# Experts: the last 96 rows of the down product, taken four tiles at a time in 32-row groups

## The chip, the core and the metric

The kernel runs on one core of a Trainium2 chip. A core has five engines with queues of their own: TensorE (PE in the profile; PEld is its weight load), VectorE (DVE), ScalarE (ACT), GpSimd (POOL) and SyncE (SP), and 16 DMA engines. The metric is the time of one execution on the device in microseconds; lower is better. The kernel before takes 3897.37 us, the median of 13 runs (3891.37 to 3909.9).

## The reference

One decoder layer in float32 on x of 32 x 128 x 512: a self-attention, a cross-attention and a mixture of experts, each with a residual. The part that matters here is the mixture. There are T = 4096 tokens of E = 512 features; each goes to 6 of 32 experts:

```python
g = jax.lax.ragged_dot(xs, w_gate, group_sizes)      # 512 -> 352, by expert
u = jax.lax.ragged_dot(xs, w_up, group_sizes)        # 512 -> 352
d = jax.lax.ragged_dot(jax.nn.silu(g) * u, w_down, group_sizes)   # 352 -> 512
expert_out = jnp.sum(out * weights[..., None], axis=1)            # out: d in token order
shared = jax.nn.silu(x @ sw_gate) * (x @ sw_up) @ sw_down
```

The contraction of the down product is over M = 352 = 128 + 128 + 96 rows. TensorE contracts over up to 128 partitions at a time, so the last piece fills 96 of them.

## The kernel before, in words

The 4096 x 6 assignments are sorted by expert into tiles of 128 tokens; `usual` = 4096 x 6 / 128 + 32 / 2 = 208 tiles are always run, and a second part for more of them stands under a condition. Class `Experts` runs them in a loop over i. There are four sets of weights (SETS = 4): tile i uses set i % 4, and a new expert's weights are loaded only if the tile's expert is new to its set (`cond=new`).

For each tile:

- `tokens` (line 1415): POOL gathers the tile's 128 token rows from DRAM in four indirect DMAs (L1421) into `e_xr` (three buffers). It is called for tile i + 5 in iteration i.
- `turn_in`: VectorE transposes them into `e_xT` (L1433), for tile i + 2 in iteration i.
- `gate_up`: TensorE makes gate and up, four matmuls each (L1446), in the two banks of one PSUM tile; there are four such PSUM tiles (`psum`, bufs=4) for the whole kernel. ACT takes Silu of gate (L1450), VectorE multiplies it by up into `e_gu` (L1451), and ACT's queue issues a DMA that writes it to DRAM (L1453).
- `part_out`: ACT's queue issues the DMA that reads it back in another layout, `e_gr` (L1462); it waits until the write has landed. A row count of 96 x 4 = 384 is kept for 352 values, the rest being zero from a memset.
- `turn_out`: VectorE transposes it into `e_guT` (L1472, two instructions: 96 partitions and 32 partitions), for tile i - 1 in iteration i.
- `down` (line 1477): TensorE makes the down product of tile i - 2 in three matmuls of 128, 128 and 96 rows (L1482) into one bank; ACT scales the result by the tokens' weights into `e_y` (L1486, two buffers); POOL adds the rows to `sum_d` in DRAM with an indirect DMA that accumulates (L1487). All these scatter-adds write the same tensor.
- `weights_in` and `weights_out`: SP's queue issues the loads of the three weights, gate and up after the tile that used the set before, the two parts of down after its down product.

The engines' queues are strictly in the order of the calls for PE, DVE, ACT and POOL (`manual_schedule` in `run`, line 1507); SP's order is a scheduler's, held by the waits. An instruction that waits holds up everything behind it in its queue. The order of calls in one iteration of the loop before is:

```python
self.gate_up(i)
self.turn_in(i + 2)
self.turn_out(i - 1)
self.weights_in(i + SETS)
self.down(i - 2)
self.weights_out(i - 2 + SETS)
self.part_out(i)
self.tokens(i + 5)
```

After the expert stage `Shared.group` runs five more groups of the shared expert; they read `sum_d` and write the output. It contains matmuls over 64 rows that stand in pairs on two halves of the partitions (L1253) after full ones (L1246). The cross-attention earlier has matmuls over 32 rows (L690 and L713).

Of the kernel before, what the change touches and what calls it, by code (L numbers as in the profile page):

```python
# [18 lines left out]
P = 128  # L19
# [1244 lines left out]
class Experts:  # L1264
# [9 lines left out]


    Q = 4
    RUN = 96

    def __init__(
        self, cm, ctx, table_ds, h3_d, sum_d, w_gate, w_up, w_down, eid, fresh, rows, n_tiles  # L1280
    ):
        self.cm, self.h3_d, self.sum_d, self.eid, self.fresh = cm, h3_d, sum_d, eid, fresh
        self.w_in, self.w_out, self.n_tiles = (w_gate, w_up), w_down, n_tiles
        nc, tc = cm.nc, cm.tc

# [12 lines left out]
        self.wd = [cp.tile([P, len(M_CHUNKS), E], F32, name=f"wd{s}") for s in range(SETS)]  # L1298

        self.gu_s = cp.tile([P, self.Q * self.RUN], F32, name="e_gu")  # L1300

        self.row_i = cp.tile([P, 2], I32, name="e_row_i")
        self.row = cp.tile([P, 2], F32, name="e_row")
        self.last, self.expert = None, {}
        self.got, self.spread = {}, {}
        self.xr, self.xT, self.gu, self.gr, self.guT = {}, {}, {}, {}, {}

    def fetch(self):
# [17 lines left out]
        nc.gpsimd.memset(self.gu_s, 0.0)  # L1326
        nc.gpsimd.iota(self.row_i, pattern=[[0, 2]], base=self.T + 1, channel_multiplier=1)

    def arrange(self, j):
# [69 lines left out]
    def weights_out(self, i):  # L1399

        if i >= self.end:
            return
        e, new = self.expert.pop(i)
        wd, src = self.wd[i % SETS], self.w_out[ds(e, 1)]
        top = (self.Q - 1) * 32
        m = (self.Q - 1) * self.RUN
        self.cm.nc.sync.dma_start(
            out=wd[0:top], in_=src[:, 0:m, :].rearrange("o (p c) m -> p (o c) m", p=top), cond=new
        )
        self.last = self.cm.nc.sync.dma_start(  # L1410
            out=wd[top:P, 0:2, :], in_=src[:, m:M, :].rearrange("o (p c) m -> p (o c) m", c=2),
            cond=new,
        )

# [23 lines left out]
    def gate_up(self, i):  # L1438
        if i >= self.end:
            return  # L1440
        nc = self.cm.nc
        pgu = self.cm.banks()
        t, s = self.xT.pop(i), i % SETS
        for half, w in enumerate((self.wg[s], self.wu[s])):
            for c in range(EC):
                nc.tensor.matmul(  # L1446
                    pgu[:, half, 0:M], t[:, c, :], w[:, c, :], start=c == 0, stop=c == EC - 1
                )
# [3 lines left out]
        self.gu[i] = self.dram.tile([self.Q, P, self.RUN], F32, name="e_gu_d")  # L1452
        nc.scalar.dma_start(  # L1453
            out=self.gu[i].rearrange("q s m -> s q m"),
            in_=self.gu_s.rearrange("s (q m) -> s q m", q=self.Q),
        )

    def part_out(self, i):


        gr = self.gr[i] = self.p2.tile([P, self.Q, self.RUN], F32, name="e_gr")
        self.cm.nc.scalar.dma_start(  # L1462
            out=gr.rearrange("p t m -> p (t m)"),
            in_=self.gu.pop(i).rearrange("q (i t) m -> (q i) (t m)", t=self.Q),
        )

    def turn_out(self, i):
        g = self.gr.pop(i)
        t = self.guT[i] = self.p2.tile([P, len(M_CHUNKS), P], F32, name="e_guT")
        top = (self.Q - 1) * 32  # L1470
        for rows, n in ((slice(0, top), 3), (slice(top, P), 2)):
            self.cm.nc.vector.transpose(  # L1472
                t[rows, 0:n, :].rearrange("p c (t i) -> p c t i", t=self.Q),
                g[rows, :, 0 : 32 * n].rearrange("p t (j c) -> p c t j", c=n),
            )

    def down(self, i):
        nc = self.cm.nc
        py = self.cm.banks()[:, 0, :]
        t, s = self.guT.pop(i), i % SETS  # L1480
        for c, (_, n) in enumerate(M_CHUNKS):
            nc.tensor.matmul(  # L1482
                py, t[:n, c, :], self.wd[s][:n, c, :], start=c == 0, stop=c == len(M_CHUNKS) - 1
            )
        y = self.p2.tile([P, E], F32, name="e_y")
        nc.scalar.mul(y, py, self.weight[:, i : i + 1])  # L1486
        nc.gpsimd.indirect_dma_start(  # L1487
            out=self.sum_d[:, :],
            out_offset=bass.IndirectOffsetOnAxis(ap=self.into[:, i : i + 1], axis=0),
# [5 lines left out]

    def begin(self, first, end):

        self.first, self.end, self.last = first, end, None
        for i in range(first, first + SETS):
            self.weights_in(i)  # L1500
            self.weights_out(i)

    def first_tokens(self):
        for i in range(self.first, self.first + 3):
# [2 lines left out]
    def run(self):  # L1507
# [3 lines left out]
        with self.cm.tc.manual_schedule(engines={en.PE, en.DVE, en.Activation, en.Pool}):  # L1511
            for i in range(first, first + 2):
                self.turn_in(i)
                self.tokens(i + 3)
            for i in range(first, self.end + 2):
                self.gate_up(i)
                self.turn_in(i + 2)
# [3 lines left out]
                if i > first + 1:  # L1521
                    self.down(i - 2)
                    self.weights_out(i - 2 + SETS)
                if i < self.end:
                    self.part_out(i)
                self.tokens(i + 5)


@with_exitstack
# [179 lines left out]
```

## Time and profile before

| what | value |
|---|---|
| median of 13 runs | 3897.37 us (3891.37 to 3909.9) |
| the profiled execution | 3896.81 us |
| its span, first to last instruction | 3895.1 us |
| granted TensorE clock, mean | 0.992 |
| PE busy in the span | 3778.8 us, 97% |
| POOL busy in the span | 2354.3 us, 60% |
| L1446, gate and up, 2 x 1664 records | 527.9 and 526.4 us |
| L1482, down, 1248 records | 570.5 us |
| L1421, gathers, x832 | 851.5 us, 1023 ns each |
| L1487, scatter-adds, x208 | 336.0 us, 1615 ns each |

A float32 matmul leaves two records in this trace: 208 tiles x 3 down matmuls are 1248 records. Busy time leaves out register, semaphore and DMA-issuing instructions, and the time an engine needs between two instructions is shown as idle time, put down to "issue". Because matmuls are pipelined, the length of a group of them is read best from the start of the next group, and not from its own length.

### The profile page before, as it was taken

To read this page: it belongs to the slowest core of one execution; us is meant where nothing else is said; L and a number is where in the kernel's file an instruction comes from. 1 tells how busy PE (TensorE), PEld (TensorE's weight loads), DVE (VectorE), ACT (ScalarE), POOL (GpSimd) and SP (SyncE) were. 2 spreads that over 40 slices of the span, in tenths; PEclk is the share of its full clock that TensorE was granted. 3 is DMA by queue.
4 is the path that set the end of the run, shared out by engine and by line. 5 is a ranking of instruction groups with operands and counts; after the bars stand their busy time and mean duration, and the time that the engine had idled before them with its cause. 6 is when DMAs were issued, how large, how long until landed. Compare 5 with 4: busy or idle time off the path is not lost. (4 is left out here: it accounts for less than half of the span.)

```text
span 3895.1 us, 58185 instructions
## 1 busy us (share of the span) xinstructions
PE 3778.8 (97%) x19060; PEld 2013.7 (52%) x19060; DVE 2056.6 (53%) x3202; ACT 1682.6 (43%) x4032; POOL 2354.3 (60%) x2582
## 2 busy tenths in 40 slices
PE   8999999989999999999999999999999999999999
PEld 5666666534444444444445555555555555555444
DVE  5788777777787777778223333333333333333111
ACT  6888888857677676776301111111111111111000
POOL 3545544545777777776336777777777777775000
PEclk9999999999999999999999999999999999999999
DMA  3111110121111111111245767676766676676210
GB/s 111 33 34 34 34 34 28 34 87 49 58 58 45 49 50 50 50 50 36 68 145 141 179 165 179 145 193 152 178 159 166 169 184 156 171 171 155 83 62 32
DMA packets 285987, 387.21 MB, mean 99 GB/s; under 512 B 147888, under 2 KB 179248, under 8 KB 285616
## 3 DMA queue, kind: packets, MB, share of 16 engines
q1 hardware_dynamic: 81792, 190.98, 15.1%
q0 software_dynamic: 62912, 109.85, 14.9%
q10 hardware_dynamic: 140976, 82.60, 7.5%
q8 instruction: 154, 2.52, 0.3%
q14 instruction: 153, 1.25, 0.1%
HBM read 617.52 MB, written 143.07 MB: 195 GB/s over the span
## 5 line engine op out<-in xcount | busy, mean ns | idle before, releaser
L1421 POOL DMA_INDIRECT e_xr<-h_d,e_run_of x832 | 851.5, 1023 | 287.2 <-issue 270.6
L694 DVE TENSOR_REDUCE nm<-ps 128x2 f32<-128x1024 f32 x512 | 611.0, 1216 | 111.9 <-PE ps L690 105.3
L717 ACT ACTIVATE xp<-ps 128x1024 f32<-128x1024 f32 x512 | 506.0, 1021 | 264.9 <-PE ps L690 203.2
L1451 DVE TENSOR_TENSOR e_gu<-e_act,ps 128x352 f32<-128x352 f32 x208 | 108.4, 521 | 947.3 <-ACT e_act L1450 624.3
L1482 PE MATMUL ps<-wd,e_guT 128*128 128x512 f32 (+1 forms) x1248 | 570.5, 593 | 6.8 <-issue 5.1
L713 PE MATMUL ps<-xqn,xk 32*128 32x512 f32 x2048 | 527.1, 620 | 20.6 <-ACT xp L717 19.2
L1446 PE MATMUL ps<-wg,e_xT 128*128 128x352 f32 x1664 | 527.9, 460 | 6.6 <-DMA wg<-in_L_ffn_w_gate_dram 6.6
L690 PE MATMUL ps<-xk,xq 32*128 32x512 f32 x2048 | 527.6, 630 | 1.1 <-DVE nm L694 1.0
L1446 PE MATMUL ps<-wu,e_xT 128*128 128x352 f32 x1664 | 526.4, 459 | 0.7 <-DMA wu<-in_L_ffn_w_up_dram 0.7
L1450 ACT ACTIVATE e_act<-ps 128x352 f32<-128x352 f32 x208 | 96.5, 464 | 922.5 <-PE ps L1446 524.6
L1446 PEld LDWEIGHTS ps<-wg,e_xT 128*128 128x128 f32 x1664 | 315.0, 190 | 241.4 <-issue 107.2
L1487 POOL DMA_INDIRECT sum_d<-e_y,e_into x208 | 336.0, 1615 | 123.9 <-issue 89.9
L1446 PEld LDWEIGHTS ps<-wu,e_xT 128*128 128x128 f32 x1664 | 316.0, 190 | 177.5 <-DMA wu<-in_L_ffn_w_up_dram 2.2
L279 ACT ACTIVATE s<-s,a_nm 128x128 f32<-128x128 f32 x1024 | 395.5, 394 | 5.2 <-DVE a_nm L265 5.2
L1482 PEld LDWEIGHTS ps<-wd,e_guT 128*128 128x128 f32 (+1 forms) x1248 | 236.6, 190 | 253.7 <-issue 212.6
L713 PEld LDWEIGHTS ps<-xqn,xk 32*128 32x128 f32 x2048 | 168.6, 183 | 284.3 <-ACT xp L717 123.3
L1486 ACT ACTIVATE e_y<-ps,e_weight 128x512 f32<-128x512 f32 x208 | 143.0, 687 | 393.7 <-PE ps L1482 289.3
L228 POOL TENSOR_SCALAR k<-kz,a_keep,a_extra 128x256 f32<-128x256 f32 x128 | 82.6, 655 | 315.7 <-ACT kz L227 315.7
L1472 DVE STREAM_TRANSPOSE e_guT<-e_gr 96x384 f32<-96x384 f32 (+1 forms) x416 | 230.3, 554 | 54.8 <-DMA e_gr<-e_gu_d 38.7
L1027 POOL DMA_INDIRECT table_d<-entry,at x192 | 202.5, 1055 | 63.5 <-issue 52.8
L728 PE MATMUL ps<-xp,v 128*32 128x512 f32 x2048 | 233.0, 595 | 7.9 <-ACT xp L717 7.9
L1433 DVE STREAM_TRANSPOSE e_xT<-e_xr 128x512 f32<-128x512 f32 x208 | 226.5, 1089 | 10.6 <-DMA e_xr<-h_d,e_run_of 10.5
(272 smaller groups left out, 5289.7 us busy)
## 6 DMA issues: line engine op xcount, KB each, us to landing
wg<-in_L_ffn_w_gate_dram SPq DMA_DIRECT2D x208, 704.0 KB
wu<-in_L_ffn_w_up_dram SPq DMA_DIRECT2D x208, 704.0 KB
wd<-in_L_ffn_w_down_dram SPq DMA_DIRECT2D x208, 576.0 KB
e_gu_d<-e_gu ACTq DMA_DIRECT2D x208, 192.0 KB
e_gr<-e_gu_d ACTq DMA_DIRECT2D x208, 192.0 KB
wd<-in_L_ffn_w_down_dram SPq DMA_DIRECT2D x208, 128.0 KB
e_xr<-h_d,e_run_of POOLq DMA_INDIRECT x832
xres<-in_x_dram SPq DMA_DIRECT2D x32, 256.0 KB
```

The costliest lines, as they stand in the source:

```text
L279: nc.scalar.activation(s[:, j, c, side, :], s[:, j, c, side, :], AF.Exp, bias=nm[n][:, side, at : at + 1], accum_out=sm[n][:, to : to + 1],)
L690: self.nc.tensor.matmul(sc[:, i, :], q[rows, ts(c, P)], k[rows, :], start=True, stop=True)
L694: self.nc.vector.tensor_reduce(at[:, self.ROW[side], 2 * pair : 2 * pair + 2], sc, AX.X, ALU.max, negate=True)
L713: self.nc.tensor.matmul(sc[:, i, :], k[rows, ts(c, P)], q[rows, :], start=True, stop=True)
L717: self.nc.scalar.activation(e, sc, AF.Exp)
L728: self.nc.tensor.matmul(po[b, side][ts(j, 32), :], self.v2[b % 2][:, c, 2 * j + side, :], es[j // 2][:, j % 2, :], start=c == 0, stop=c == ...
L1421: self.cm.nc.gpsimd.indirect_dma_start(out=xr[:, t, :], out_offset=None, in_=self.h3_d.rearrange("t (q f) -> (t q) f", q=self.Q), in_offse ...
L1433: self.cm.nc.vector.transpose(xT.rearrange("p c (t i) -> p c t i", t=self.Q), self.xr.pop(i).rearrange("p t (j c) -> p c t j", c=EC),)
L1446: nc.tensor.matmul(pgu[:, half, 0:M], t[:, c, :], w[:, c, :], start=c == 0, stop=c == EC - 1)
L1472: self.cm.nc.vector.transpose(t[rows, 0:n, :].rearrange("p c (t i) -> p c t i", t=self.Q), g[rows, :, 0 : 32 * n].rearrange("p t (j c) -> ...
L1482: nc.tensor.matmul(py, t[:n, c, :], self.wd[s][:n, c, :], start=c == 0, stop=c == len(M_CHUNKS) - 1)
L1487: nc.gpsimd.indirect_dma_start(out=self.sum_d[:, :], out_offset=bass.IndirectOffsetOnAxis(ap=self.into[:, i : i + 1], axis=0), in_=y[:, :] ...
```

## The change

The first 256 rows of the down product stay per tile, as two full matmuls of 128 rows. The last 96 rows (`END` = 256, `LEFT` = 96) are laid on 32 partitions in three chunks: tile i uses the 32 partitions of its lane, i % 4, in three new tiles shared by four tiles: `wd_ends` (weights), `e_lr` (gate times up, read back) and `e_endT` (transposed). When the fourth tile of a group has had its two full matmuls (or at the end), `ends_down` does three rounds, one for each chunk, of four matmuls, one for each tile, each on its own 32 partitions and into its own bank. Until then the four tiles keep their banks: two PSUM tiles of two banks each.

What follows from it in the other queues:

- ACT's queue issues four DMAs per tile around `e_gu` in place of two: the 256 columns and the 96 columns are written and read back separately. There is no padding and no memset any more.
- VectorE transposes 128 partitions (256 columns) and 32 partitions (384 columns) in place of 96 and 32.
- SP loads the down weights as 256 rows (`weights_out`) and, after the group's last round, 96 rows for each of four tiles (`ends_in`).
- Scaling and scatter-add are taken out of `down` into `leave`. It is called up to twice in an iteration, from the list `done` of tiles whose product is complete: once between `part_out` and `tokens`, once after `tokens`. So the four tiles of a group leave in two iterations, two in each; in the other two iterations none leaves.

```diff
-    RUN = 96
+    RUN = 64
+    END, LEFT = 256, 96
...
-        self.wd = [cp.tile([P, len(M_CHUNKS), E], F32, name=f"wd{s}") for s in range(SETS)]
-
-        self.gu_s = cp.tile([P, self.Q * self.RUN], F32, name="e_gu")
+        self.wd = [cp.tile([P, self.END // P, E], F32, name=f"wd{s}") for s in range(SETS)]
+        self.ends = cp.tile([P, self.LEFT // 32, E], F32, name="wd_ends")
+        self.lr = cp.tile([P, self.Q, self.LEFT], F32, name="e_lr")
+        self.gu_s = cp.tile([P, M], F32, name="e_gu")
...
+    def ends_in(self, i):
+        if i >= self.end:
+            return
         e, new = self.expert.pop(i)
...
+            out=self.ends[ts(i % SETS, 32)],
+            in_=self.w_out[ds(e, 1)][:, self.END : M, :].rearrange("o (p c) m -> p (o c) m", p=32),
             cond=new,
...
         nc.scalar.dma_start(
-            out=self.gu[i].rearrange("q s m -> s q m"),
-            in_=self.gu_s.rearrange("s (q m) -> s q m", q=self.Q),
-        )
+            out=top.rearrange("q s m -> s q m"),
+            in_=self.gu_s[:, 0 : self.END].rearrange("s (q m) -> s q m", q=self.Q),
+        )
+        nc.scalar.dma_start(out=left, in_=self.gu_s[:, self.END : M])
...
+        lr = self.lr
+        self.cm.nc.scalar.dma_start(
+            out=lr[ts(i % SETS, 32)].rearrange("p t m -> p (t m)"),
+            in_=left.rearrange("(i t) m -> i (t m)", t=self.Q),
+        )
...
     def down(self, i):
         nc = self.cm.nc
-        py = self.cm.banks()[:, 0, :]
-        t, s = self.guT.pop(i), i % SETS
-        for c, (_, n) in enumerate(M_CHUNKS):
+        lane = i % SETS
+        if lane % 2 == 0:
+            self.py[i // 2] = self.cm.banks()
+        t, _ = self.guT[i]
+        for c in range(self.END // P):
             nc.tensor.matmul(
-                py, t[:n, c, :], self.wd[s][:n, c, :], start=c == 0, stop=c == len(M_CHUNKS) - 1
-            )
+                self.py[i // 2][:, lane % 2, :], t[:, c, :], self.wd[lane][:, c, :],
+                start=c == 0, stop=False,
+            )
+
+    def ends_down(self, tiles):
+        last = self.LEFT // 32 - 1
+        for c in range(last + 1):
+            for i in tiles:
+                rows = ts(i % SETS, 32)
+                self.cm.nc.tensor.matmul(
+                    self.py[i // 2][:, i % 2, :], self.guT[i][1][rows, c, :], self.ends[rows, c, :],
+                    start=False, stop=c == last,
+                )
+
+    def leave(self, i):
+        nc = self.cm.nc
+        py = self.py[i // 2][:, i % 2, :]
+        del self.guT[i]
         y = self.p2.tile([P, E], F32, name="e_y")
         nc.scalar.mul(y, py, self.weight[:, i : i + 1])
+        if i % 2 or i == self.end - 1:
+            del self.py[i // 2]
         nc.gpsimd.indirect_dma_start(
...
+            done = []
             for i in range(first, self.end + 2):
...
                 if i > first + 1:
                     self.down(i - 2)
                     self.weights_out(i - 2 + SETS)
+                    if (i - 1) % SETS == 0 or i == self.end + 1:
+                        group = range((i - 2) // SETS * SETS, i - 1)
+                        self.ends_down(group)
+                        for n in group:
+                            self.ends_in(n + SETS)
+                        done += group
                 if i < self.end:
                     self.part_out(i)
+                if done:
+                    self.leave(done.pop(0))
                 self.tokens(i + 5)
+                if done:
+                    self.leave(done.pop(0))
+            for i in done:
+                self.leave(i)
```

More of the change, by code (lines that the diff above doesn't have):

```diff
@@ L1306, in __init__ @@
         self.xr, self.xT, self.gu, self.gr, self.guT = {}, {}, {}, {}, {}
+        self.py, self.endT = {}, None
     def fetch(self):
@@ L1325, in fetch @@
                 )
-        nc.gpsimd.memset(self.gu_s, 0.0)
         nc.gpsimd.iota(self.row_i, pattern=[[0, 2]], base=self.T + 1, channel_multiplier=1)
@@ L1402, in weights_out @@
             return
-        e, new = self.expert.pop(i)
[L1404 to L1408, printed above, removed]
-        )
+        e, new = self.expert[i]
+        self.last = self.cm.nc.sync.dma_start(
+            out=self.wd[i % SETS],
+            in_=self.w_out[ds(e, 1)][:, 0 : self.END, :].rearrange("o (p c) m -> p (o c) m", p=P),
+            cond=new,
+        )
+    def ends_in(self, i):
+        if i >= self.end:
+            return
+        e, new = self.expert.pop(i)
         self.last = self.cm.nc.sync.dma_start(
-            out=wd[top:P, 0:2, :], in_=src[:, m:M, :].rearrange("o (p c) m -> p (o c) m", c=2),
+            out=self.ends[ts(i % SETS, 32)],
+            in_=self.w_out[ds(e, 1)][:, self.END : M, :].rearrange("o (p c) m -> p (o c) m", p=32),
             cond=new,
@@ L1451, in gate_up @@
         nc.vector.tensor_tensor(self.gu_s[:, 0:M], act, pgu[:, 1, 0:M], ALU.mult)
-        self.gu[i] = self.dram.tile([self.Q, P, self.RUN], F32, name="e_gu_d")
+        top = self.dram.tile([self.Q, P, self.RUN], F32, name="e_gu_d")
+        left = self.dram.tile([P, self.LEFT], F32, name="e_left_d")
+        self.gu[i] = top, left
         nc.scalar.dma_start(
-            out=self.gu[i].rearrange("q s m -> s q m"),
-            in_=self.gu_s.rearrange("s (q m) -> s q m", q=self.Q),
+            out=top.rearrange("q s m -> s q m"),
+            in_=self.gu_s[:, 0 : self.END].rearrange("s (q m) -> s q m", q=self.Q),
         )
+        nc.scalar.dma_start(out=left, in_=self.gu_s[:, self.END : M])
     def part_out(self, i):
-        gr = self.gr[i] = self.p2.tile([P, self.Q, self.RUN], F32, name="e_gr")
+        top, left = self.gu.pop(i)
+        gr = self.p2.tile([P, self.Q, self.RUN], F32, name="e_gr")
         self.cm.nc.scalar.dma_start(
             out=gr.rearrange("p t m -> p (t m)"),
-            in_=self.gu.pop(i).rearrange("q (i t) m -> (q i) (t m)", t=self.Q),
+            in_=top.rearrange("q (i t) m -> (q i) (t m)", t=self.Q),
         )
-    def turn_out(self, i):
[L1468 to L1471, printed above, removed]
+        lr = self.lr
[3 more added lines that the diff above has]
+        )
+        self.gr[i] = gr, lr
+    def turn_out(self, i):
+        gr, lr = self.gr.pop(i)
+        lane = i % SETS
+        if lane == 0 or self.endT is None:
+            self.endT = self.p2.tile([P, self.LEFT // 32, P], F32, name="e_endT")
+        t = self.p2.tile([P, self.END // P, P], F32, name="e_guT")
+        self.guT[i] = t, self.endT
+        rows = ts(lane, 32)
+        for to, g in ((t, gr), (self.endT[rows], lr[rows])):
             self.cm.nc.vector.transpose(
-                t[rows, 0:n, :].rearrange("p c (t i) -> p c t i", t=self.Q),
-                g[rows, :, 0 : 32 * n].rearrange("p t (j c) -> p c t j", c=n),
+                to.rearrange("p c (t i) -> p c t i", t=self.Q),
+                g.rearrange("p t (j c) -> p c t j", j=32),
             )
@@ L1478, in down @@
         nc = self.cm.nc
-        py = self.cm.banks()[:, 0, :]
-        t, s = self.guT.pop(i), i % SETS
-        for c, (_, n) in enumerate(M_CHUNKS):
+        lane = i % SETS
+        if lane % 2 == 0:
+            self.py[i // 2] = self.cm.banks()
+        t, _ = self.guT[i]
+        for c in range(self.END // P):
             nc.tensor.matmul(
-                py, t[:n, c, :], self.wd[s][:n, c, :], start=c == 0, stop=c == len(M_CHUNKS) - 1
-            )
+                self.py[i // 2][:, lane % 2, :], t[:, c, :], self.wd[lane][:, c, :],
+                start=c == 0, stop=False,
+            )
+    def ends_down(self, tiles):
[11 more added lines that the diff above has]
+        del self.guT[i]
         y = self.p2.tile([P, E], F32, name="e_y")
         nc.scalar.mul(y, py, self.weight[:, i : i + 1])
+        if i % 2 or i == self.end - 1:
+            del self.py[i // 2]
         nc.gpsimd.indirect_dma_start(
@@ L1496, in begin @@
     def begin(self, first, end):
-        self.first, self.end, self.last = first, end, None
+        self.first, self.end, self.last, self.endT = first, end, None, None
         for i in range(first, first + SETS):
@@ L1501, in begin @@
             self.weights_out(i)
+            self.ends_in(i)
     def first_tokens(self):
```

## The prediction, made before the result was known

> **What bounds the kernel now.** I read first the page's row of engines, then the timeline of TensorE in the middle of the expert stage, then POOL's timeline there and at the stage's end.
>
> ```profile
> PE 3778.8 (97%) x19060; PEld 2013.7 (52%) x19060; DVE 2056.6 (53%) x3202; ACT 1682.6 (43%) x4032; POOL 2354.3 (60%) x2582
> ```
>
> TensorE is busy for 97% of the span, and in the expert stage (208 tiles, about 2070 to 3601 us) its timeline has no gap. Columns: start, length, engine, line, operation. A float32 matmul leaves two records, so x6 are the three matmuls of one down product.
>
> ```profile
> 2810.38 2.53 PE L1446 MATMUL ps<-wg,e_xT 128*128 128x352 f32 x8
> 2812.74 2.53 PE L1446 MATMUL ps<-wu,e_xT 128*128 128x352 f32 x8
> 2815.11 2.74 PE L1482 MATMUL ps<-wd,e_guT 128*128 128x512 f32 x6
> 2817.69 2.53 PE L1446 MATMUL ps<-wg,e_xT 128*128 128x352 f32 x8
> ```
>
> From gate to gate is 2817.69 - 2810.38 = 7.31 us per tile: 4.73 for gate and up, 2.58 for three down matmuls, 0.86 each; the third takes as long as the others although it has 96 rows. Four tiles take 4 x 7.31 = 29.24 us. So TensorE sets the pace. But POOL, at 60%, is not free: issue time between its instructions isn't counted as busy. Its timeline, mid-stage and at the end:
>
> ```profile
> 2804.23 1.62 POOL L1487 DMA_INDIRECT sum_d<-e_y,e_into  x1 [0.36 <-issue]
> ...
> 2811.54 1.61 POOL L1487 DMA_INDIRECT sum_d<-e_y,e_into  x1 [0.38 <-issue]
> ```
>
> ```profile
> 3561.48 1.61 POOL L1487 DMA_INDIRECT sum_d<-e_y,e_into  x1 [0.67 <-issue]
> 3563.40 1.06 POOL L1421 DMA_INDIRECT e_xr<-h_d,e_run_of  x1 [0.30 <-issue]
> ...
> 3568.72 1.62 POOL L1487 DMA_INDIRECT sum_d<-e_y,e_into  x1 [0.30 <-issue]
> 3575.07 1.58 POOL L1487 DMA_INDIRECT sum_d<-e_y,e_into  x1 [4.73 <-issue]
> 3580.57 1.55 POOL L1487 DMA_INDIRECT sum_d<-e_y,e_into  x1 [3.92 <-issue]
> ...
> 3599.70 1.55 POOL L1487 DMA_INDIRECT sum_d<-e_y,e_into  x1 [4.05 <-issue]
> 3605.26 1.55 POOL L1487 DMA_INDIRECT sum_d<-e_y,e_into  x1 [4.01 <-issue]
> ```
>
> POOL does one scatter-add (L1487) and four gathers (L1421) per tile. 3561.48 to 3568.72 is such a cycle with only the 0.3 us issue gap before its scatter: 7.24 us. So POOL has 0.07 us of slack per tile, and no more. Second reading: where two scatters stand together with no gathers between, the second starts 6.35 us (3568.72 to 3575.07), 5.50 (3575.07 to 3580.57) and 5.56 us (3599.70 to 3605.26) after the first. Both add into `sum_d`, so the second waits in POOL's queue until the first has landed.
>
> **The change part by part.** *The product on TensorE.* Removed per four tiles: four 96-row matmuls, 4 x 0.86 = 3.44 us. Added: three rounds of four 32-row matmuls into four different banks. Do four row groups run side by side? The cross attention has 32-row matmuls of two lines standing together:
>
> ```profile
> 1400.33 0.70 PE L713 MATMUL ps<-xqn,xk 32*128 32x512 f32 x2
> 1400.34 0.70 PE L690 MATMUL ps<-xk,xq 32*128 32x512 f32 x2
> 1400.86 0.59 PE L713 MATMUL ps<-xqn,xk 32*128 32x512 f32 x2
> 1400.87 1.01 PE L690 MATMUL ps<-xk,xq 32*128 32x512 f32 x4
> 1401.30 0.59 PE L713 MATMUL ps<-xqn,xk 32*128 32x512 f32 x2
> 1401.72 0.59 PE L690 MATMUL ps<-xk,xq 32*128 32x512 f32 x2
> 1401.73 0.59 PE L713 MATMUL ps<-xqn,xk 32*128 32x512 f32 x2
> ```
>
> Sixteen records of 0.43 us (6.9 in series) are over in 1.99 us: four at a time, plus a start of about 0.1. Changing the tiling costs something; the chain that ended last has it in the shared expert:
>
> ```profile
> 3649.04 1.06 PE ps L1253 x4
> 3650.10 8.78 PE ps L1246 x20
> ```
>
> Two 64-row matmuls side by side should take 2 x 0.43 = 0.86; they take 1.06, and the 20 full records after them 8.78 instead of 20 x 0.429 = 8.58. Way in and back: 0.40 us. So the three rounds take 3 x 0.86 + 0.40 = 2.98, TensorE's group is 29.24 - 3.44 + 2.98 = 28.78, and the gain on TensorE alone is 0.46 x 52 groups = 24 us. Bounds for 52 groups: with no cost of switching, 0.86 x 52 = 45 us gained; in series, 12 x 0.86 + 0.40 - 3.44 = 7.3 per group, 378 us lost. I take 0.46, since both neighbouring rows show groups side by side.
>
> The Trainium skill, TensorE: Matmul & The Clock Gate, section "Part 3: Packing small matmuls", gives 3.07 times as measured for four-way row packing with 32 rows and 512 columns. By it (an estimate) the rounds would take 12 x 0.86 / 3.07 + 0.40 = 3.76 us, and TensorE would lose 0.3 us per group, 17 us in all; the cross attention's rows here show 6.9 / 1.99 = 3.4 with the start in it.
>
> *POOL: scatters moved.* The work is the same, the order is not. Before: scatter, four gathers, scatter, four gathers. After, `leave` runs once before and once after `tokens` in the two iterations from a group's end on: scatter 0, four gathers, scatter 1 | scatter 2, four gathers, scatter 3 | four gathers | four gathers. Scatter 2 stands directly behind scatter 1, and its wait for scatter 1's landing has no work ahead of it that could cover it. Queued behind it are the gathers of the tile five ahead, for which `turn_in` on VectorE, then gate and up on TensorE, wait. So once in every group POOL idles as at the stage's end. From 1.92 us (3561.48 to 3563.40, scatter to next instruction) the step becomes 5.50 to 6.35. A lower bound from mid-stage: asked for line 1487 there, POOL's queue shows waits for the landings of the scatters of 2804.23 and 2826.16 that end at 2809.07 and 2830.87, 4.84 and 4.71 after their starts; the tail's queue wait that began at 3599.6 and lasted 5.00 ended about 0.70 before the scatter at 3605.26, so 4.71 + 0.70 = 5.4. These scatters, like scatter 1, came behind four gathers, but so did the one of 6.35. I take the mean of the three steps, 5.80, and keep 5.4 and 6.35 for the range.
>
> POOL's group: 4 x 7.24 = 28.96, less 1.92, plus 5.80 = 32.84 us. That is longer than TensorE's 28.78, and POOL's order does not let it catch up: POOL becomes the bound. Against 29.24 it is 3.60 us more per group. Gathers are called five tiles ahead and turned two ahead, so some lateness is hidden at first; POOL falls behind by 32.84 - 28.78 = 4.1 us per group, and a lead of about one tile (7.3 us) is gone in two groups; the first group has no scatter ahead of it. That leaves 49 of 52: 49 x 3.60 = 176 us.
>
> *ACT.* Per tile two DMA issues more, about 0.36 each by the 0.37 and 0.34 of the two that exist; ACT is busy 63 of 400 us mid-stage (busy times by stretch, 2800 to 3200). New waits: the scaling of a leaving tile now stands behind `part_out`, which waits for both writes of gate-times-up, and `e_y` has two buffers, so `leave` of tile 3 waits until scatter 1 has landed. Behind it on ACT stands the next Silu, then on VectorE the product, `turn_in` and `turn_out`, then the down product of lane 2. From scatter 1 to the next group's scatter 1 this loop is: landing 5.1, scale 0.69, Silu 0.46 with its handover 0.51, product 0.53, transposes 1.09 and 0.63, then TensorE 1.72 + 4.73 + 1.72 + 2.58, scale and handover 1.3, scatter and gathers 7.24, in all 27.8 us, under 32.84: it decides where TensorE stands idle (at the down product of lane 2, about 32.8 - 28.8 = 4 us a group), not how long the group is. If it grew by more than 5 us it would.
>
> *The rest, at nothing.* Two transposes per tile remain two (1.11 us together on VectorE, busy 139 of 400 us; if the 32 x 384 one took 1.1 alone there is still cover). SP issues as many weight transfers, 16 per group, of the same bytes; `ends_in` moves four of them behind the group's last round, and they are next read a group later; if that cover were gone they would show as TensorE waits on `wd_ends`. The banks of a pair are held longer, but gate and up wait for one freed about 5 us earlier. One memset goes. At the end the last four scatters stand together, 3 x 5.5 us later than TensorE, ahead of the last groups' loads of `sum_d`; those are first added at 3650 (the chain above), some 45 us after the last scatter now, so this is hidden.
>
> *Sum.* The profiled execution took 3896.81 us (span 3895.1, 1.7 around it), 0.6 below the median 3897.37. 3896.8 + 176 = 4073 us. The gain of 24 us on TensorE disappears in its new idle time.
>
> The Trainium skill, DMA: Bandwidth & Descriptors, section "Anatomy of one DMA — SWDGE (gpsimd) path", puts a transfer at about 2.0 us plus bytes / 436 GB/s. For the scatter's 256 KB that is 2.6; with the 1.6 us of the instruction and 0.7 of restart (an estimate) the step would be 4.9, and the sum 3896.8 + 49 x 2.7 = 4029. The tail's steps here, 5.50 and more, speak for the longer one.
>
> **Rivals.**
> 1. *No new wait* (the other side). If scatter 1 had landed when POOL comes to scatter 2, the group would be POOL's 28.96: 0.28 x 52 = 15 us faster, 3882. It decides if landing takes under 1.9 us; every pair of neighbours in the tail speaks against. 5%.
> 2. *Row groups in series.* TensorE's group 29.24 + 7.3 = 36.5, POOL's wait hidden under it: 3896.8 + 378 = 4275. Both rows of side-by-side groups speak against; only the order, four tiles inside each chunk, is not shown. 4%.
> 3. *The ACT loop closes.* If waits for landings, weight loads and DMA issues add over 5 us to the loop of 27.8, groups of 34 to 36 follow: 49 x (4.8 to 6.8) more, 4130 to 4230. For it: ACT's queue now holds waits of three kinds; against: the 5 us. 8%.
> 4. *No difference* would need POOL and TensorE to meet at 29.24 by chance: 2%.
>
> **How the numbers follow.** The forecast has 81%. Its own bounds: step 5.4 gives (28.96 - 1.92 + 5.4 - 29.24) = 3.2; with ten groups hidden instead of three, 42 x 3.2 = 134, so 4031. Step 6.35 in all 52 groups: 52 x 4.15 = 216, so 4113. The range is 4031 to 4130: from that lower bound to where rival 3 begins, since a small part of rival 3 can come on top of a short step; it leaves out the rivals and little else. No change means within 0.2% (8 us), about what a measurement of this kernel can tell. Faster 5% (rival 1), same 2%, slower 93%.
>
> **What the profile after would show.** POOL's timeline: once in four tiles two scatters 5.4 to 6.4 us apart with nothing between, and no idle time elsewhere; groups of 32 to 33.5 us from gate to gate. TensorE: twelve 32-row matmuls in about 2.6 us, and some 4 us idle a group ahead of a down product, put down to `e_guT`. TensorE's share falls to about 93%. I am wrong if the two scatters stand 2 us apart (rival 1), or if POOL idles elsewhere and TensorE waits for ACT (rival 3).

## The result, and the profile after

The changed kernel takes 4139.4 us, the median of 8 runs (4133.9 to 4156.7), against 3900.1 for the kernel before on the same chip: 1.0622 times as long, 95% interval 1.0610 to 1.0634, 239 us more. I had put it at 4073, in a range of 4031 to 4130. The direction and the place were right, the size was too small. Four lines of the profile after, engines first:

```profile
PE 3834.0 (93%) x19892; PEld 2012.6 (49%) x19892; DVE 2049.5 (50%) x3202; ACT 1667.5 (40%) x4032; POOL 2347.5 (57%) x2581
...
L1508 PE MATMUL ps<-wd,e_guT 128*128 128x512 f32 x832 | 446.7, 664 | 183.6 <-DVE e_guT L1495 94.9
...
L1533 POOL DMA_INDIRECT sum_d<-e_y,e_into x208 | 333.2, 1602 | 365.8 <-ACT e_y L1530 289.5
...
L1530 ACT ACTIVATE e_y<-ps,e_weight 128x512 f32<-128x512 f32 x208 | 135.8, 685 | 741.5 <-DMA e_left_d<-e_gu 154.5
```

TensorE falls from 97% to 93%. Nearly all of its idle time in the expert stage, 183.6 us, stands ahead of the down product (L1508), and most of POOL's, 365.8 us, ahead of the scatter-adds (L1533). POOL's timeline, mid-stage:

```profile
2813.74 1.62 POOL L1533 DMA_INDIRECT sum_d<-e_y,e_into  x1 [2.06 <-ACT e_y L1530]
...
2820.97 1.61 POOL L1533 DMA_INDIRECT sum_d<-e_y,e_into  x1 [0.30 <-issue]
2828.49 1.56 POOL L1533 DMA_INDIRECT sum_d<-e_y,e_into  x1 [5.90 <-ACT e_y L1530]
...
2835.72 1.62 POOL L1533 DMA_INDIRECT sum_d<-e_y,e_into  x1 [0.30 <-issue]
...
2848.20 1.62 POOL L1533 DMA_INDIRECT sum_d<-e_y,e_into  x1 [0.30 <-issue]
```

This is one group: scatters 0, 1, 2, 3 and the next 0. Between scatters 1 and 2 there is nothing, and POOL sits for 5.90 us. That is the predicted idle place. In this group the step from scatter 1 to scatter 2 is 7.52 us, one of the longer ones; the median is 5.78. The second idle place, 2.06 us ahead of scatter 0, was not predicted. Averages over 48 groups in mid-stage, start to start:

| step | predicted (by its sum) | after, mean (median) | the same kernel on another chip, mean (median) |
|---|---|---|---|
| scatter 0 to 1 | 7.24 | 7.27 (7.24) | 7.46 (7.24) |
| scatter 1 to 2 | 5.80 | 6.35 (5.78) | 5.81 (5.61) |
| scatter 2 to 3 | 7.24 | 7.30 (7.24) | 7.22 (7.24) |
| scatter 3 to the next 0 | 12.56 | 13.00 (12.87) | 12.53 (12.49) |
| group | 32.84 | 33.93 (33.73) | 33.02 (32.72) |

Where the 237.7 us between the two profiled spans lie, by the starts of the gate products of tiles 0, 16 and 200: before tile 0, -5.4; tiles 0 to 15, 120.7 against 111.9, +8.8; tiles 16 to 199, 1567.6 against 1361.2, +206.4, or 4.49 in each of 46 groups (I had 3.60); from tile 200 to the end, 389.3 against 361.3, +28.0 (I had two groups, 7.2). So two terms are missing: 0.9 us per group, and some 21 us at the end.

The end can be read off TensorE's timeline, first of the kernel after, then of the kernel before. L1519 are the row-tile rounds, L1214 is the first matmul of the shared expert.

```profile
3819.05 1.98 PE L1508 MATMUL ps<-wd,e_guT 128*128 128x512 f32 x4 [3.26 <-DVE e_guT L1495]
3820.96 2.86 PE L1519 MATMUL ps<-wd_ends,e_endT 32*128 32x512 f32 x24
3838.60 5.17 PE L1214 MATMUL ps<-s_hT,sg 128*128 128x512 f32 x8 [14.78 <-ACTq L1703]
```

```profile
3597.99 2.82 PE L1482 MATMUL ps<-wd,e_guT 128*128 128x512 f32 x6 [2.31 <-issue]
3602.43 3.67 PE L1214 MATMUL ps<-s_hT,sg 128*128 128x512 f32 x8 [1.63 <-PEq L1643]
```

TensorE waits 14.78 us for ACT's queue to reach L1703, the condition that ends the stage, where it waited 1.63 before. ACT is late because the scaling of the last two tiles waits for the landings of scatters (two `e_y` buffers); a run of set C shows it.

The other missing term shows in mid-stage, first on TensorE, then on ACT and on POOL (L1455 is gate and up, L1459 their Silu):

```profile
2840.84 2.86 PE L1519 MATMUL ps<-wd_ends,e_endT 32*128 32x512 f32 x24
2843.63 2.63 PE L1455 MATMUL ps<-wg,e_xT 128*128 128x352 f32 x8
2846.10 2.53 PE L1455 MATMUL ps<-wu,e_xT 128*128 128x352 f32 x8
2848.47 1.88 PE L1508 MATMUL ps<-wd,e_guT 128*128 128x512 f32 x4
2850.19 2.53 PE L1455 MATMUL ps<-wg,e_xT 128*128 128x352 f32 x8
2852.55 2.53 PE L1455 MATMUL ps<-wu,e_xT 128*128 128x352 f32 x8
2860.05 3.78 PE L1508 MATMUL ps<-wd,e_guT 128*128 128x512 f32 x4 [4.97 <-DVE e_guT L1495]
2863.63 3.41 PE L1455 MATMUL ps<-wg,e_xT 128*128 128x352 f32 x8
```

```profile
2845.46 1.26 ACT L1530 ACTIVATE e_y<-ps,e_weight 128x512 f32<-128x512 f32 x2 [5.71 <-issue]
2857.67 0.46 ACT L1459 ACTIVATE e_act<-ps 128x352 f32<-128x352 f32 x1 [10.94 <-remote]
...
2861.96 1.27 ACT L1530 ACTIVATE e_y<-ps,e_weight 128x512 f32<-128x512 f32 x2 [3.83 <-DMA e_left_d<-e_gu]
```

```profile
2855.44 1.61 POOL L1533 DMA_INDIRECT sum_d<-e_y,e_into  x1 [0.30 <-issue]
2862.93 1.56 POOL L1533 DMA_INDIRECT sum_d<-e_y,e_into  x1 [5.88 <-ACT e_y L1530]
```

The gate and up products of 2843.63 and 2846.10 are over at about 2848.6. Their Silu waits for nothing but TensorE's signal, ACT has nothing ahead of it, and yet it starts at 2857.67, nine microseconds late. In the trace's semaphore events, four updates of TensorE come together at 2857.59 to 2857.83, and in the same stretch SP's plain register instructions last 0.7 us each, where they usually take 0.02 to 0.15. POOL, which had run without a pause, had finished its last instruction at 2857.05. Two things follow. The scaling of tile 2 stands in ACT's queue behind `part_out`, which waits for the write of that Silu's result; it starts at 2861.96, and scatter 2 right behind it, 7.49 us after scatter 1. And on VectorE the transpose for lane 1 stands behind the same result, so TensorE idles 4.97 us ahead of lane 1's down product. Its next matmuls run at half the speed (3.78 us for the four records that took 1.88, 3.41 for eight that took 2.53); the granted clock is 0.50 from 2858.6 to 2865.4.

### The profile page after: what moved, and what is told of

Read it like the earlier page. It is cut to its first block, busy times and chain, and to the rows that moved or that the text cites. A ratio compares the mean times of both kernels' runs of the same rounds, so it can differ in the third digit from the quotient of the medians.

```text
span 4132.8 us, 60612 instructions
## 1 busy us (share of the span) xinstructions
PE 3834.0 (93%) x19892; PEld 2012.6 (49%) x19892; DVE 2049.5 (50%) x3202; ACT 1667.5 (40%) x4032; POOL 2347.5 (57%) x2581
## 5 line engine op out<-in xcount | busy, mean ns | idle before, releaser
L1508 PE MATMUL ps<-wd,e_guT 128*128 128x512 f32 x832 | 446.7, 664 | 183.6 <-DVE e_guT L1495 94.9
L1455 PE MATMUL ps<-wg,e_xT 128*128 128x352 f32 x1664 | 552.0, 476 | 1.6 <-ACT e_y L1530 0.9
L1533 POOL DMA_INDIRECT sum_d<-e_y,e_into x208 | 333.2, 1602 | 365.8 <-ACT e_y L1530 289.5
L1455 PE MATMUL ps<-wu,e_xT 128*128 128x352 f32 x1664 | 526.2, 459 | 0.0
L1455 PEld LDWEIGHTS ps<-wg,e_xT 128*128 128x128 f32 x1664 | 327.0, 199 | 274.6 <-issue 137.2
L1459 ACT ACTIVATE e_act<-ps 128x352 f32<-128x352 f32 x208 | 96.0, 462 | 825.5 <-PE ps L1455 253.7
L1455 PEld LDWEIGHTS ps<-wu,e_xT 128*128 128x128 f32 x1664 | 316.2, 190 | 176.1
L1508 PEld LDWEIGHTS ps<-wd,e_guT 128*128 128x128 f32 x832 | 164.9, 205 | 363.6 <-issue 214.8
L279 ACT ACTIVATION_READ_ACCUMULATOR s<-s,a_nm 128x1 f32 x1024 | 198.1, 193 | 0.0
```

Source lines behind the costliest of these rows:

```text
L279: nc.scalar.activation(s[:, j, c, side, :], s[:, j, c, side, :], AF.Exp, bias=nm[n][:, side, at : at + 1], accum_out=sm[n][:, to : to + 1],)
L1455: nc.tensor.matmul(pgu[:, half, 0:M], t[:, c, :], w[:, c, :], start=c == 0, stop=c == EC - 1)
L1508: nc.tensor.matmul(self.py[i // 2][:, lane % 2, :], t[:, c, :], self.wd[lane][:, c, :], start=c == 0, stop=False,)
L1533: nc.gpsimd.indirect_dma_start(out=self.sum_d[:, :], out_offset=bass.IndirectOffsetOnAxis(ap=self.into[:, i : i + 1], axis=0), in_=y[:, :] ...
```

## The experiments

Fifteen runs of eleven kernels were made, in four sets; the runs of a set shared a chip, and each is compared with the kernel before on that chip, which took 3939.6 us in set A, 3884.4 in B, 3884.3 in C and 3942.6 in D. Two things are counted in every trace, because they bear on the term that was missing in mid-stage: how late the Silu of lane 2 (i % 4 == 2, the first tile after the rounds) starts on average, counted from 0.55 us after the start of the last up matmul, and how many of SP's instructions in the stage (2100 to 3500 us) lasted 0.48 to 0.76 us ("slow" below). In the runs of the result these are 4.65 us and 302 for the kernel after, 0.65 us and 278 for the kernel before.

### Set A: which part costs what

**Three buffers for the scaled tile.**

```diff
-        y = self.p2.tile([P, E], F32, name="e_y")
+        y = self.p2.tile([P, E], F32, name="e_y", bufs=3)
```

(To make room for the third buffer, a table of row numbers is cut to the part that is used, and a small tile of the set-up shares another's buffer.)

> The changed kernel with three e_y buffers in place of two, so that the scaling of a group's fourth tile no longer waits on ACT for the landing of scatter 1; scatter 2 stands directly behind scatter 1 as before. If POOL's step from scatter 1 to scatter 2 (median 5.78 us) is all that counts: within 10 us of 4139. If the waits of ACT for that landing close the loop of ACT (groups of 33.9 us against POOL's own 32.8): 49 x 1.1 = 54 us less, 4075 to 4095. If what is late is the signal of TensorE after its row-tile rounds (posted 1 to 9 us late in the trace), which this does not touch: some of it stays, 4110 to 4139.

Measured: 4132.1 us, 1.0490 (1.0466 to 1.0513). Groups of 33.63 us; scatter 1 to 2 has a median of 5.87, so POOL's step is what it was. Lane 2's Silu is 5.85 us late, with 348 slow instructions on SP: the lateness is there with a third buffer too. How much they win can't be told from this set, since the changed kernel itself did not run on this chip.

**One leaving tile in each iteration**, so that no two scatters are neighbours:

```diff
                 self.tokens(i + 5)
-                if done:
-                    self.leave(done.pop(0))
             for i in done:
                 self.leave(i)
```

> The changed kernel with one leaving tile in each iteration in place of two in two of four iterations; no scatter stands behind another without four gathers between. If the neighbouring scatters are the cause: POOL's group is 4 x 7.24 = 28.96 us, TensorE's 28.78, so (28.96 - 29.24) x 52 = -15 us against the kernel before, about 3885. If TensorE's late signals or ACT's queue count by themselves: groups of 29.5 to 31 us, 3910 to 3990. If the row-tile rounds or the extra DMAs are the cause, and not the scatters: above 4000.

Measured: 4064.1 us, 1.0323 (1.0288 to 1.0358), by its number the third case. Without neighbours 125 us are still lost here; set C shows that this hangs on the chip, and takes that conclusion back. Groups of 32.37 us, and the idle time ahead of a scatter is 0.9 to 2.0 us on average, by its place in the group. Lane 2's Silu is 2.16 us late, and 264 of SP's instructions are slow.

**The pair alone**, in the kernel before: the scatter is taken out of `down` and, in every fourth iteration, put behind the gathers.

```diff
...
-                self.tokens(i + 5)
+                if i > first + 1 and i % SETS != 3:
+                    self.scatter(i - 2)
+                self.tokens(i + 5)
+                if i > first + 1 and i % SETS == 3:
+                    self.scatter(i - 2)
```

> The kernel before, with nothing changed but that in every fourth iteration the scatter goes behind that iteration's gathers, so that it stands directly ahead of the next one: one pair of neighbours per four tiles, as in the changed kernel, without row tiles, new DMAs or grouped leaving. By the prediction's sum: 49 x 3.60 = 176 us more, 4073; with steps of 5.4 to 6.35 us 4031 to 4113. If the pair alone makes all of what the change cost: 4139. If it costs nothing: 3897.

Measured: 4058.4 us, 1.0302 (1.0278 to 1.0325). POOL's timeline of this run:

```profile
2812.09 1.61 POOL L1493 DMA_INDIRECT sum_d<-e_y,e_into  x1 [0.30 <-issue]
2817.44 1.56 POOL L1493 DMA_INDIRECT sum_d<-e_y,e_into  x1 [3.74 <-ACT e_y L1487]
...
2824.69 1.62 POOL L1493 DMA_INDIRECT sum_d<-e_y,e_into  x1 [0.30 <-issue]
```

The step is 5.35 us here, 5.87 on average, and the group is 32.86 us; the prediction's sum for POOL was 32.84. The absolute time is close to 4073 as well. One pair in four tiles makes POOL the bound, with no row tile and no new DMA in the kernel. On this chip the kernel before is itself 43 us slower than the 3897 that the sum started from, so the difference is 119 us and not 176. There are 306 slow instructions on SP. Lane 2's Silu is 4.0 us late, but behind ACT's own queue: counted from the end of what stands ahead of it there, it is 0.16 us late (4.23 in the kernel after).

**Grouped leaving with the product of before**, which has the same `leave` and order as the changed kernel, but three full matmuls per tile:

```diff
-        py = self.cm.banks()[:, 0, :]
+        if i % 2 == 0:
+            self.py[i // 2] = self.cm.banks()
+        py = self.py[i // 2][:, i % 2, :]
...
```

> The kernel before's product (128, 128 and 96 rows per tile, its DMAs and transposes), but the four tiles of a group keep their banks and leave as in the changed kernel, two in each of two iterations. If the rest of the loss (4139 against the predicted 4073) comes from ACT's waits for landings with two e_y buffers: 4120 to 4145. If it comes from the row-tile rounds, their late signals or the new DMAs: 4065 to 4085.

Measured: 4101.4 us, 1.0416 (1.0392 to 1.0441), between the two cases. Groups of 33.07 us, scatter 1 to 2 5.80 on average. So of 162 us, 119 come with the pair, and the other 43, if the two simply add, with leaving in groups. Lane 2's Silu is 1.87 us late, with 326 slow instructions on SP.

### Set B: another chip

**The changed kernel again.**

> The changed kernel once more, beside the three others on the same chip. If chips differ only by a common factor, its ratio to the kernel before is 1.062 again; if the ratio hangs on the chip (the kernel before took 3940 us on the one of the last runs), 1.05 to 1.06.

Measured: 4088.9 us, 1.0524 (1.0506 to 1.0541), 205 us more than before. The chips do not differ by a common factor. On this one 23 of SP's instructions are slow and not 302, lane 2's Silu is 0.27 us late and not 4.65, and POOL's groups are 33.02 us, close to the predicted 32.84. A group of it on POOL:

```profile
2826.39 1.62 POOL L1533 DMA_INDIRECT sum_d<-e_y,e_into  x1 [0.30 <-issue]
...
2833.63 1.61 POOL L1533 DMA_INDIRECT sum_d<-e_y,e_into  x1 [0.30 <-issue]
2839.13 1.56 POOL L1533 DMA_INDIRECT sum_d<-e_y,e_into  x1 [3.89 <-ACT e_y L1530]
...
2846.37 1.62 POOL L1533 DMA_INDIRECT sum_d<-e_y,e_into  x1 [0.30 <-issue]
```

Scatter 0 no longer waits, and scatter 2 starts 5.50 us after scatter 1.

**The product of before in groups, one leaving tile in each iteration** (the two edits above together): neither neighbours nor row tiles nor new DMAs.

> The kernel before's product (128, 128 and 96 rows per tile, its DMAs and transposes), in groups of four that keep their banks, one tile leaving in each iteration: neither neighbouring scatters nor row tiles nor new DMAs. If the 127 us that were left with one leaving tile an iteration come from the row-tile rounds or the new DMAs: within 20 us of the kernel before. If they come from keeping four tiles back (banks, ACT's order): 80 to 130 us more than before.

Measured: 3921.1 us, 1.0097 (1.0076 to 1.0119). The 37 us more lie a little outside the first case; 15 of them are the end: L1214 starts 17.2 us after the last down matmul's start, against 2.2 in the kernel before.

**The loads of `wd_ends` one in each iteration**, with one leaving tile in each iteration:

```diff
-                        for n in group:
-                            self.ends_in(n + SETS)
                         done += group
+                        late += [n + SETS for n in group]
+                    if late:
+                        self.ends_in(late.pop(0))
...
```

> The changed kernel with one leaving tile in each iteration (as in the run that took 1.032 times the kernel before), and the four loads of wd_ends of a group issued one in each iteration in place of four in a row behind the rounds. If SP's bunch of issues, which stands in the trace beside the late signals of TensorE, is the cause: most of the 127 us go, ratio 1.00 to 1.012. If SP's bunch is only a fellow sufferer: no change, 1.028 to 1.036.

Measured: 3918.3 us, 1.0080 (1.0062 to 1.0098). By its number this is the first case, but the comparison was with the chip of set A; set C takes that conclusion back.

**ACT's DMAs of the kernel before split in two**, nothing else:

```diff
-        nc.scalar.dma_start(
-            out=self.gu[i].rearrange("q s m -> s q m"),
-            in_=self.gu_s.rearrange("s (q m) -> s q m", q=self.Q),
-        )
+        for h in (slice(0, 2), slice(2, 4)):
+            nc.scalar.dma_start(
+                out=self.gu[i].rearrange("q s m -> s q m")[:, h],
+                in_=self.gu_s.rearrange("s (q m) -> s q m", q=self.Q)[:, h],
+            )
```

(The read is split in the same way.)

> The kernel before with each of ACT's two DMAs per tile (the write of e_gu and the read of e_gr) split into two halves, the same bytes and packets: four issues on ACT as in the changed kernel, and nothing else. If the number of DMA issues beside POOL's running descriptors is what makes signals late: 80 to 130 us more than before. If it costs only ACT's 0.7 us per tile, which is hidden: within 10 us of before.

Measured: 3897.4 us, 1.0032 (1.0015 to 1.0050), 13 us. Four issues on ACT per tile cost little on a chip without late signals. What they cost on the other kind was not tried.

### Set C: the end, and everything put right

**The changed kernel once more**, as the measure for this set:

> The changed kernel again, as the measure for the next three on this chip. Where the trace shows TensorE's signals late (on the first chip its fourth of four tiles' Silu started 4.7 us late on average, on the third chip 0.3 us), ratio 1.06 and groups of 33.9 us; where it does not, 1.052 and 33.0.

(The expectation says "fourth of four tiles"; the numbers are those of lane 2, the third.) Measured: 4090.9 us, 1.0528 (1.0512 to 1.0544), 26 slow instructions on SP, lane 2 late by 0.24 us, groups of 33.11.

**Loads spread, and the last two tiles of the run scaled into `e_xT` buffers**, which are free by then:

```diff
-        y = self.p2.tile([P, E], F32, name="e_y")
+        y = self.p2.tile([P, E], F32, name="e_xT" if i >= self.end - 2 else "e_y")
...
-                        for n in group:
-                            self.ends_in(n + SETS)
                         done += group
+                        late += [n + SETS for n in group]
+                if late:
+                    self.ends_in(late.pop(0))
```

> The changed kernel with two edits that act in different places. One: the four loads of wd_ends one in each iteration and not in a row. Two: the last two tiles of the whole run scale into free e_xT buffers, so that ACT doesn't wait for the landings of the last scatters. The second by itself: the first matmul of the shared expert (L1214) follows the last down product by 3 to 4 us and not by 15 to 18, and the time from tile 200 to the end falls by 11 us. The first: if SP's bunch makes signals late, groups of 33.9 become 33.0 on a chip that shows them; on one that does not, no change (within 0.1 us per group).

Measured: 4089.2 us, 1.0521 (1.0505 to 1.0537). TensorE and ACT at the end:

```profile
3787.27 2.86 PE L1519 MATMUL ps<-wd_ends,e_endT 32*128 32x512 f32 x24
3792.76 5.40 PE L1214 MATMUL ps<-s_hT,sg 128*128 128x512 f32 x8 [2.63 <-ACTq L1704]
```

```profile
3790.24 1.27 ACT L1530 ACTIVATE e_y<-ps,e_weight 128x512 f32<-128x512 f32 x2 [12.46 <-PE ps L1519]
3791.40 1.27 ACT L1530 ACTIVATE e_xT<-ps,e_weight 128x512 f32<-128x512 f32 x2
```

All four scalings now run without waiting for a landing, TensorE idles 2.63 us and not 14.78, and the time from tile 200 to the end is 375.7 us against 387.8, as expected, 12.1 less. The scatters still follow one another until 3809, and nothing that sets the end waits for them. The spread loads don't help here: groups of 33.25 us. Ahead of tile 200 some 7 us are lost again (2.0 before tile 0, 4.1 over tiles 0 to 15, 1.0 over tiles 16 to 199), so that the two profiled spans differ by 5.0 us, and the two medians by 1.7 only.

**One leaving tile in each iteration**, the kernel of set A, on this chip:

> One leaving tile in each iteration again (1.032 on the second chip), beside the changed kernel on one chip. If the late signals made most of that: 1.01 on a chip whose trace does not show them, 1.03 on one that does. If the loads of wd_ends in a row cost by themselves: 1.02 to 1.03 on any chip.

Measured: 3922.1 us, 1.0100 (1.0085 to 1.0116), where it was 1.0323 in set A. 41 slow instructions on SP, lane 2 late by 0.14 us. Against the changed kernel on this chip it is 169 us less, of the 207 that the change cost here: 3.2 us for each of 52 groups. So on a chip without late signals the neighbouring scatters make most of the loss. The loads in a row cost nothing to speak of by themselves: 3918.3 with them spread, against 3884.4; 3922.1 with them in a row, against 3884.3, on two chips of the same kind.

**Everything put right**: three `e_y`, scalings two and two, one scatter in each iteration, loads spread, the end as above.

```diff
...
+                for n in done[:2]:
+                    self.leave(n)
+                done = done[2:]
+                if self.y:
+                    self.scatter(min(self.y))
                 self.tokens(i + 5)
...
```

> Everything put right that the runs named: three e_y buffers, a group's tiles scaled two in each of two iterations but one scatter in every iteration ahead of its gathers, the loads of wd_ends one in each iteration, the last two tiles scaled into free e_xT buffers. POOL's group 4 x 7.24 = 28.96 us against 29.24: if that is what is left, 0.28 x 52 = 15 us under the kernel before less a few at the end, ratio 0.996 to 1.000. If hiccups that POOL can't win back count (mean groups of 29.6 as in the last run with one leaving tile): 1.003 to 1.006.

Measured: 3893.1 us, 1.0022 (1.0011 to 1.0032). All but 9 us of the loss is gone, and nothing is won. The median group is 28.99 us, which is POOL's 28.96, but the mean is 29.54, as in the kernel before (29.55 on the first chip). My reading is that where a scatter waits, POOL has no slack to win it back; no run tests it.

### Set D: what makes late signals hurt

**One leaving tile in each iteration**, as the measure:

> One leaving tile in each iteration, as the measure for the next two on this chip: ratio 1.03 where the trace shows TensorE's and SP's signals late (over 200 of SP's instructions of about 0.7 us in the stage), 1.01 where it does not (under 50).

Measured: 4070.1 us, 1.0332 (1.0309 to 1.0356); 233 slow instructions, lane 2 late by 2.94 us. This is the kind of chip of set A.

**The product of before in groups**, the kernel that was 1.0097 in set B:

> The kernel before's product in groups of four, one leaving tile in each iteration, no row tiles, no new DMAs (1.010 on the third chip). On a chip with late signals: 1.03 if grouping and POOL's missing slack are enough for the loss, about 1.01 if it takes the row-tile rounds or the new loads and DMAs. On one without: 1.010 again.

Measured: 4006.1 us, 1.0171 (1.0124 to 1.0218); 257 slow, lane 2 late by 1.17 us.

**Loads spread, the end put right, one leaving tile in each iteration:**

> One leaving tile in each iteration, the loads of wd_ends one in each iteration, the last two tiles of the run scaled into free e_xT buffers. On a chip with late signals: about 1.01 if SP's bunch of loads makes them hurt, 1.03 if not. On one without: 1.008 less 12 us at the end, 1.003 to 1.006; under 1.000 only if POOL's groups come down to their 28.96 us on average (29.4 to 29.6 so far).

Measured: 4047.8 us, 1.0269 (1.0250 to 1.0288); 180 slow, lane 2 late by 2.00 us. Against the measure of this set it wins 22 us, 12 of which the end would give by itself. SP's loads in a row are at most a small part.

What TensorE waits for in one and the same kernel (one leaving tile in each iteration) in sets C and D, by waits from 2180 to 3660 us, the columns being total, times and longest; C first:

```profile
...
PE ps L1455 <- DVE e_gu L1460: 16.1, 11, 3.9
PE ps L1455 <- ACT e_y L1530: 7.7, 4, 4.0
...
```

```profile
PE ps L1455 <- DVE e_gu L1460: 74.3, 24, 8.3
PE ps L1455 <- issue: 49.4, 21, 10.0
...
```

TensorE's gate product waits for a PSUM tile that the previous tile's product (`e_gu`) has to free; two of the four PSUM tiles are held by tiles that wait for their group. In the run with the full product in set D the first of these rows is 32.0 us. That row is there without row tiles too, so the held banks let late signals reach TensorE, as these waits read; what the row tiles bring costs more still (1.0269 with the end and the loads put right, against 1.0171 without either edit). No run changed the late signals by themselves: chips with and without them are compared, and another difference between chips isn't ruled out. Which of the row-tile rounds, their signals or ACT's new DMAs it is stays open.

## Why the prediction was right, and where it was wrong

*TensorE's product: right.* TensorE in set D, with one leaving tile in each iteration, where a stretch ran without waits:

```profile
2816.37 2.86 PE L1519 MATMUL ps<-wd_ends,e_endT 32*128 32x512 f32 x24
2819.16 2.63 PE L1455 MATMUL ps<-wg,e_xT 128*128 128x352 f32 x8
...
2825.71 2.53 PE L1455 MATMUL ps<-wg,e_xT 128*128 128x352 f32 x8
...
2832.16 2.53 PE L1455 MATMUL ps<-wg,e_xT 128*128 128x352 f32 x8
...
2845.15 2.86 PE L1519 MATMUL ps<-wd_ends,e_endT 32*128 32x512 f32 x24
```

From one set of rounds to the next it is 2845.15 - 2816.37 = 28.78 us, the predicted figure. A tile without rounds takes 6.45 (2832.16 - 2825.71), so the rounds cost 28.78 - 4 x 6.45 = 2.98 us, way in and back included. The row groups run side by side (rival 2 is out). The factor of 3.07 that the Trainium skill gives in TensorE: Matmul & The Clock Gate, "Part 3: Packing small matmuls", would have made it 3.76 (an estimate); the trace decides for 2.98.

*POOL's step: right.* 5.80 was taken, the median is 5.78 on the first chip and 5.61 on the other; with the pair alone the group is 32.86 against 32.84. Rival 1 (no new wait) is out. The 4.9 us (an estimate) worked out from the Trainium skill's DMA: Bandwidth & Descriptors, "Anatomy of one DMA — SWDGE (gpsimd) path", is too short by 0.7 to 0.9; how much of the step is the landing was not measured apart. TensorE's share is 93%, as said. It idles 3.5 us a group ahead of down products (183.6 / 52), in two places: 1.4 on average ahead of lane 2's, which was predicted with 4, and 1.9 ahead of lane 1's, behind the late Silu. On the chip of set B it is 2.8 ahead of lane 2's and nothing ahead of lane 1's.

*The end: wrong.* "This is hidden", I wrote of the last four scatters. Their landings are hidden indeed, but not the scalings on ACT that wait for them with two `e_y` buffers; behind those stands the condition at L1703, and TensorE can't start the shared expert before ACT has come through. It cost 14.78 - 1.63 = 13.2 us, and giving the last two scalings buffers of their own took most of it away (2.63 us left). The other 8 of the some 21 us at the end stay open. The term was set to zero because I followed who reads `sum_d`, and not who stands in ACT's queue.

*ACT's way to scatter 2: left without a price.* The prediction named that a leaving tile's scaling stands behind `part_out`, but summed only the loop that goes through scatter 1's landing and tile 3 (27.8 us, 5 us under POOL's group). What grew is another way, to tile 2: the rounds, lane 2's gate and up, its Silu, the write, `part_out`, the scaling of tile 2. On the first chip TensorE's signal to that Silu comes up to ten microseconds late. In 12 of the 48 groups scatter 2 starts 0.28 us after its scaling ends, on average 7.67 us after scatter 1 and not 5.8, and in 11 of these 12 lane 2's Silu is 8 to 10 us late. In the other 36 the step is 5.91 us on average. Scatter 0 waits some 2 us in many groups. That is the 0.9 us per group, 41 us over tiles 16 to 199: rival 3 in part, on top of the forecast. On the chip of set B no scatter 2 of the 48 stands right behind its scaling, the groups are 33.02 us, and this term is nearly gone. With the end's 21 us it makes 62 of the 66 us that the forecast was too low.

*The baseline.* I compared POOL's 32.84 with TensorE's undisturbed 29.24. The mean of the kernel before is 29.59 (7.398 per tile over tiles 16 to 199), so the added time ought to have been 3.25 plus such disturbances as the new order has itself. On the chip of set B, between the starts of gate products, these are about 0.4 us (33.22 a group over tiles 16 to 199, against 32.84). Two errors of about 0.35 per group cancel here, which was luck.

*The range.* Its top stood where rival 3 began, on the thought that only a small part of it could come on top. With the end's 13 us the same kernel is at 4089 to 4091 on the second kind of chip, inside the range, and at 4139 on the first. Part of that is the chip's: the kernel before takes 3884 there. The added time, 205 to 207 us, lies inside the 134 to 233 that the range allows over 3897, and 239 on the first chip does not.

## What to carry to other kernels

Two writers of one DRAM tensor that become neighbours in a queue cost their landing time in full (here 5.8 us in place of 1.9, once in four tiles); count what stands between them after the change, and not only the work. Two engines within 1% of each other (28.78 and 28.96 here) left nothing to win from either. At the end of a stage follow every queue up to the next condition or barrier: a wait that no data needs can still hold the engine that goes on.

## What the runs showed of the hardware that was not expected

- Chips differ in kind and not only in speed. The kernel before takes 3884, 3900 and 3940 us, and the same change costs 1.052 times on one and 1.062 on another; one leaving tile an iteration costs 1.010 and 1.033.
- On two of the three kinds, signals come late, mostly while POOL runs indirect DMAs without a pause. In the first chip's trace of the changed kernel, between 2150 and 3560 us, 298 of SP's 3598 instructions took 0.48 to 0.76 us. Of the 435 that ended more than 1 us into one of POOL's idle times of over 2 us, 5 did. Of the 546 intervals between TensorE's semaphore updates, 69 are close to 0.7 or 1.4 us, and on the quiet chip none of 660 is. In the group shown above the backlog goes when POOL pauses. On the quiet chip 23 of 3722 were slow under the same program. What POOL has to do with it is a guess from this coincidence; no run tested it by itself, and why chips differ is open.
- Short regular pauses cost TensorE its clock. In the kernel after, between 2080 and 3800 us, a stretch of matmuls at half speed followed 31 of TensorE's 32 idle times of over 3 us, and 4 of the 23 of 0.8 to 3 us (3.78 us in place of 1.88 in the timeline above, where the granted clock is 0.50). From 2180 to 3560 us the granted clock is 0.95 on average, and 1.00 in the kernel before. Of the gate and up records from 2080 to 3700 us, 57 of 3042 took over 0.7 us in the kernel after and 4 of 3271 in the kernel before.
